# Weight scalings placed behind a unit's copies, down weights' steps and S4 operands moved, in a gated feed-forward and S4 kernel

## The chip, the cores and the metric

The kernel runs on one core of a Trainium2 chip. The metric is the time of one execution in microseconds (us) on the device. A core has engines with queues of their own: PE (TensorE, matmuls; PEld are its weight loads), DVE (VectorE), ACT (ScalarE), POOL (GpSimd) and SP (SyncE, which here only issues DMA transfers). Each works through its instructions in order, and semaphores tie them together. Matmuls write to eight PSUM banks, all else lies in SBUF.

## The reference

The input is x with 2048 tokens of 1024 values. With xn = layernorm(x) the output is x + S4(xn) + FFN(xn).

```python
Wg, Wu, Wd = (dequantize(q, scale, zero) for q, scale, zero in ...)   # int4, groups of 64
def dequantize(W_q, scale, zero):
    w = stack([W_q >> 4 & 15, W_q & 15], axis=-1).reshape(out, 2 * half)
    return (w.reshape(out, -1, 64) - zero[:, :, None]) * scale[:, :, None]

g = einsum('bsh,ih->bsi', xn, Wg)          # hidden 1024 -> 2752
u = einsum('bsh,ih->bsi', xn, Wu)
ffn = einsum('bsi,hi->bsh', silu(g) * u, Wd)   # 2752 -> 1024

# S4: a kernel K of length 1024 from 64 complex states (Cauchy sums at the roots of unity), then
y = irfft(rfft(xn, n=2048) * rfft(K, n=2048))[..., :1024] + D * xn    # causal convolution along the hidden axis
```

## The kernel before, in words

Every float32 operand is split into a high and a low float16 part, and a product is three matmul passes (high by low, low by high, high by high). The big products go through a 2 by 2 block scheme of seven products instead of eight (`PROD` names the operands' combinations).

**First stage, to about 133 us.** Sixteen tiles of x are normalised (`norm_stat`, `norm_hi`, `norm_lo`), combined into the scheme's sums (`combine`), and the first two blocks of gate and up weights are used without the scheme (`gate_up_plain`).

**Gate-and-up loop, about 133 to 883 us.** Blocks j = 2 to 20, in two halves of the tokens, cp = 0 and 1. A *unit* is one `gate_up(j, cp)` (line 595), 38 in all, in the order (2,0), (3,0), (2,1), (3,1), (4,0), (4,1), and so on to (20,1). It is seven products of twelve 128x512 matmuls. Their order on PE is 1, 7, then product 4 of the unit before (`rest(0)`), 6, then product 3 of the unit before (`rest(1)`), 2, 5. Between them ACT makes copies from bank to bank that start the next sums: B<-A after product 1 (line 617; `heads`), hb<-C after 7, D<-B after 6, a silu in place on A after 2, and one on the D of the unit before. Product 6 can't start before B<-A is done, product 5 not before D<-B. `tails` holds the DVE addition after product 5; `lag(n)` makes a generator wait until n further units have been written down.

**Weights.** A *granule* gi is half of a block's gate and up weights; block j has 2j and 2j+1. `load_w` (line 409) takes one through: `unpack` (DMA of packed rows `raw` and of scales and zeros `sz`, two DVE shifts into `w`), `scale_c` (three POOL operations on `sz`), `scale_a` (16 ACT instructions of 128x64, one for each group: w times scale plus bias; 0.43 us each in the mean), `sums` (four DVE operations), `w_hi` (two ACT casts to `nat`), `w_lo` (two DVE subtractions) and `w_t` (two transposing DMAs from SP, wf<-nat). In the loop there is one buffer for `w`, there are two for `sz`, four for `raw`, five for `nat`, four for `wf` (two blocks). Granules 4 to 7 are traced ahead of the loop, 8 to 41 in it; granule 4's unpacking is tied behind the last norm operation of tile 13 (`BEHIND`). `w_scale` cuts the 16 scalings into 5, 6 and 5, all tied behind the B<-A copy of one unit. Two further granules (`G_WP`) hold the last 64 columns' down weights.

**Down weights.** `load_wd(u)` (line 460), ten generators of some eleven steps, prepares them for the second stage; it fetches packed rows and transposed scales (w<-SZT), dequantises on DVE (`dequant`), and makes seven combinations `nd` (ACT cast, DVE subtraction, DMA store WD<-nd). The loop takes four steps after each pass (j, cp) from j = 4 on.

**S4.** The generator `s4()` builds K in the same loop, two or three steps a pass from j = 4. `s4_cauchy(qt)` (line 736), run four times, fetches cosine and sine rows (s4n<-in_csrow) into a `nat` buffer, works on them with DVE up to a reciprocal and multiplies on PE (s4s).

**Second stage, from 883 us.** The S4 convolution (cv, cc) and the last tiles, then the down product in the seven-product scheme (A, D, E with operands g and b).

**Order.** The program is traced, and a planner that simulates the time lays out each engine's queue: what was traced earlier goes first among what is ready by its reckoning. `issue_after(ins)` adds that the instructions in its block stand behind `ins` on that engine; it places nothing directly behind it. Ahead of the loop, DVE, ACT and SP work in an order written out by hand ("pinned").

Of the kernel before, what the change touches and what calls it, by code (L numbers as in the profile page):

```python
# [42 lines left out]
G_WP = G_WD + 2 * NPAIR  # L43


S4_FROM, WD_FROM = 4, 4


SPG = 8
FETCH = {8: 15, 9: 15}  # L50
BEHIND = {4: 13}

XS = 64.0
WS = 1024.0
# [33 lines left out]
def build(nc, tc, x, xp, raw_d, sz_d, par_d, vct_d, tab_d, csrow_d, out):  # L88
# [3 lines left out]
    with es:  # L92
# [193 lines left out]


        with ea:
            slots, heads, tails, ends = {}, {}, [], [None]
            rawt = {}  # L290

            def load_raw(gi):
# [27 lines left out]
            def scale_c(gi, sz):  # L320

                G.tensor_scalar(sz[:, 0], sz[:, 0], WS, None, ALU.mult)  # L322
                G.tensor_tensor(sz[:, 1], sz[:, 1], sz[:, 0], ALU.mult)
                G.tensor_scalar(sz[:, 1], sz[:, 1], -1.0, None, ALU.mult)
                return sz

            def scale_a(w, sc, groups=range(16)):

                wv = w.rearrange("p a b -> p (a b)")
                for g in groups:  # L330
                    A.activation(
                        wv[:, 64 * g : 64 * g + 64], wv[:, 64 * g : 64 * g + 64].bitcast(I32), AF.Identity,
                        bias=sc[:, 1, g : g + 1], scale=sc[:, 0, g : g + 1],
                    )
# [46 lines left out]
                w, sz = unpack(gi)  # L381
                made[gi] = w, scale_c(gi, sz)

            def w_scale(gi, part, behind=None):
                with tc.issue_after(heads[behind].ins) if behind in heads else nullcontext():
                    scale_a(*made[gi], range((0, 5, 11)[part], (5, 11, 16)[part]))

            def w_sums(gi):
                sums(made[gi][0], False)
# [16 lines left out]
                    last[0] = SP.dma_start_transpose(wf[:, 14 * k : 14 * k + 14], nat.rearrange("p a b c -> p (a b c)"))  # L406
                wt.setdefault(gi // 2, []).append(wf)

            def load_w(gi, behind=None):
                if gi in BEHIND:  # L410
                    with tc.issue_after(los[BEHIND[gi]].ins):
                        w, sz = unpack(gi)
                    made[gi] = w, scale_c(gi, sz)
                else:
                    w_unpack(gi)
                for part in range(3):
                    w_scale(gi, part, behind)
                w_sums(gi)
                w_hi(gi)
                w_lo(gi)  # L420
                w_t(gi)


            def wp_hi(i):
                made[G_WP + i] = made[G_WP + i][0], wtemp("nat", [P, 1024], F16, f"wph{i}")
                w, hi = made[G_WP + i]
                A.copy(hi, w.rearrange("p a b -> p (a b)")[:, :1024])

            def wp_lo(i):
                w, hi = made.pop(G_WP + i)  # L430
                lo = wtemp("nat", [P, 1024], F16, f"wpl{i}")
                V.tensor_tensor(lo, w.rearrange("p a b -> p (a b)")[:, :1024], hi, ALU.subtract)
                SP.dma_start(WPN[:, i, 0:1024], hi)
                SP.dma_start(WPN[:, i, 1024:2048], lo)

            def scales_t():

# [22 lines left out]
            def load_wd(u):  # L460
# [51 lines left out]
                    ready_wd[ga] = fetch_wd(ga)  # L512
                    yield
                ready_wd[gb] = fetch_wd(gb)
                yield from lag(2 if u == 0 else 1)
                ma = ready_wd.pop(ga)
                with tc.issue_after(tails[-1].ins):
                    dequant(*ma)
# [73 lines left out]

            pending = []

            def gate_up(j, cp, wf):

                def prod(i, ps, start, stop):
                    fa, fb = PROD[i]
                    xt = xtile(cp, fb)
                    for kt in range(4):  # L600
                        for n, (wi, xi) in enumerate(PASS):
                            ends[0] = PE.matmul(
                                ps, wf[kt // 2][:, 14 * (kt % 2) + 2 * fa + wi, :], xt[:, xi, kt, :],
                                start=(start and kt == 0 and n == 0), stop=(stop and kt == 3 and n == 2),
                                skip_group_check=not start,
                            )

                def rest(i):
                    if len(pending) > i:
                        pending[i]()  # L610

                nm = f"{j}_{cp}"
                isc = 1.0 / (XS * WS)
                add, mult = ALU.add, ALU.mult
                bA, bB = bank("A" + nm), bank("B" + nm, "B")
                prod(1, bA, True, True)
                heads[j, cp] = A.copy(bB, bA)
                bC = bank("C" + nm)
                prod(7, bC, True, True)
                tag = "h" if j % 2 else "e"  # L620
                hb = htile("hb_" + nm, tag)
                A.copy(hb, bC)
                rest(0)
                prod(6, bB, False, True)
                bD = bank("D" + nm, "D")
                A.copy(bD, bB)
                rest(1)
                pending.clear()
                prod(2, bA, False, True)
                A.activation(bA, bA, AF.Silu, scale=isc)  # L630
                prod(5, bD, False, True)
                tails.append(V.tensor_tensor(hb, bD, hb, add))

                def fourth():
                    prod(4, bC, False, True)
                    ha = htile("ha_" + nm, tag)
                    A.copy(ha, bC)
                    V.tensor_tensor(ha, bB, ha, add)
                    V.scalar_tensor_tensor(ha, ha, HS * isc, bA, mult, mult)
                    pending[1] = lambda: third(ha)  # L640

                def third(ha):
                    prod(3, bD, False, True)
                    A.activation(bD, bD, AF.Silu, scale=isc)
                    V.scalar_tensor_tensor(hb, hb, HS * isc, bD, mult, mult)
                    finish_h(j, cp, ha, hb)

                pending.extend((fourth, None))
# [87 lines left out]
            def s4_cauchy(qt):  # L736

                work = wtemp("nat", [P, 3, 256], F32, f"s4n{qt}")
                cs, sn, di = (work[:, i] for i in range(3))
                re, im = slice(0, 64), slice(64, 128)  # L740
                SP.dma_start(cs, csrow_d[0, 256 * qt : 256 * qt + 256].partition_broadcast(P))
                SP.dma_start(sn, csrow_d[1, 256 * qt : 256 * qt + 256].partition_broadcast(P))
                yield
                V.tensor_scalar(sn, sn, sm[:, 28:29], None, ALU.mult)
                V.scalar_tensor_tensor(di, cs, sm[:, 30:31], sn, ALU.mult, ALU.add)
                V.tensor_scalar(cs, cs, sm[:, 29:30], None, ALU.mult)
                yield
                V.tensor_tensor(sn, cs, cs, ALU.mult)
                for rows, d2 in ((re, di), (im, cs)):
                    V.tensor_tensor(d2[rows], di[rows], di[rows], ALU.mult)  # L750
                    V.tensor_tensor(sn[rows], sn[rows], d2[rows], ALU.add)
                yield
                V.reciprocal(sn, sn)
                V.tensor_tensor(sn[re], cs[re], sn[re], ALU.mult)
                V.scalar_tensor_tensor(sn[im], di[im], -1.0, sn[im], ALU.mult, ALU.mult)
                yield from lag()
                rr = sn.rearrange("p (a b) -> p b a", b=8)
                ps = bank(f"s4s{qt}")
                rows = slice(32 * qt, 32 * qt + 32)
                with tc.issue_after(ends[0].ins):  # L760
                    for l1 in range(8):
                        PE.matmul(ps[rows, 8 * l1 : 8 * l1 + 8], rr[:, l1, :], cf, start=True, stop=True)
                yield
                V.tensor_copy(s4p[rows, 48:112], ps[rows, 0:64])
                yield
# [220 lines left out]
            wd_steps = (None for u in range(NPAIR) for _ in load_wd(u))  # L986
            s4_steps = s4()

            gate_up(2, 0, wt[2])
            gate_up(3, 0, wt[3])  # L990
            for j in range(2, NJ):
                if 3 <= j < NJ - 1:
                    load_w(2 * j + 2, (j - 1, 1))
                    load_w(2 * j + 3, (j - 1, 1))
                for cp in range(2):
                    if cp or j > 3:
                        gate_up(j, cp, wt[j])
                    for _ in range(4 if j >= WD_FROM else 0):
                        next(wd_steps, 0)
                    for _ in range(3 - cp if j >= S4_FROM else 0):  # L1000
                        next(s4_steps, 0)
                if j == NJ - 2:
                    for i in range(2):
                        w_unpack(G_WP + i)
                        for part in range(3):
                            w_scale(G_WP + i, part)
                        wp_hi(i)
                        wp_lo(i)
            settle()
            for steps in (wd_steps, s4_steps):  # L1010
                for _ in steps:
# [393 lines left out]
```

## Time and profile before

| what | us |
|---|---|
| median of three runs (1336.7 to 1338.47) | 1338.17 |
| profiled execution, its own time | 1336.8 |
| its span, first to last instruction | 1335.0 |
| TensorE busy | 1277.1 |
| VectorE busy | 991.1 |
| ScalarE busy | 669.1 |
| mean granted TensorE clock | 0.987 |
| ACT scalings w<-w,sz, 640 | 217.1 |

In a row of a timeline the first number is the start in us from the span's start, the second the duration in us; then come engine, operation, written and read tiles, shapes, the number of instructions merged, and in brackets the idle time of the engine just ahead and what ended it ("issue": nothing that the profile can name). A row of the waits has the total in us, how often, and the longest. Idle time of an engine matters only where TensorE comes to wait for it.

### The profile page before, as it was taken

To read this page: it belongs to the slowest core of one execution; us is meant where nothing else is said; L and a number is where in the kernel's file an instruction comes from. 1 tells how busy PE (TensorE), PEld (TensorE's weight loads), DVE (VectorE), ACT (ScalarE), POOL (GpSimd) and SP (SyncE) were. 2 spreads that over 40 slices of the span, in tenths; PEclk is the share of its full clock that TensorE was granted. 3 is DMA by queue.
4 is the path that set the end of the run, shared out by engine and by line. 5 is a ranking of instruction groups with operands and counts; after the bars stand their busy time and mean duration, and the time that the engine had idled before them with its cause. 6 is when DMAs were issued, how large, how long until landed. Compare 5 with 4: busy or idle time off the path is not lost. (4 is left out here: it accounts for less than half of the span.)

```text
span 1335.0 us, 20888 instructions
## 1 busy us (share of the span) xinstructions
PE 1277.1 (96%) x7880; PEld 751.0 (56%) x7880; DVE 991.1 (74%) x1344; ACT 669.1 (50%) x1208; POOL 189.7 (14%) x267
## 2 busy tenths in 40 slices
PE   6999799999999989989989999999999999999998
PEld 5644344444444434434433444456557888888887
DVE  7759986568797787779668687662738897779792
ACT  4777457647664745557466756720204433443330
POOL 3220010100000100111001001000000022255540
PEclk8999899999999998999999999999999999999999
DMA  6792947459896988699789979695937779799991
GB/s 224 181 189 52 218 137 137 124 142 234 193 257 160 236 204 226 156 226 239 185 222 226 242 191 223 201 281 183 329 132 296 259 201 270 241 260 265 288 189 50
DMA packets 358400, 276.02 MB, mean 207 GB/s; under 512 B 211668, under 2 KB 304668, under 8 KB 354204
## 3 DMA queue, kind: packets, MB, share of 16 engines
q1 hardware_dynamic: 335676, 261.59, 71.4%
q0 software_dynamic: 21760, 10.49, 6.6%
q10 hardware_dynamic: 864, 2.62, 0.6%
q8 instruction: 61, 1.00, 0.3%
q14 instruction: 39, 0.32, 0.1%
HBM read 132.36 MB, written 94.84 MB: 170 GB/s over the span
## 5 line engine op out<-in xcount | busy, mean ns | idle before, releaser
L77 PEld LDWEIGHTS <-wf 128*128 128x128 f16 x3960 | 374.1, 99 | 473.7 <-issue 40.6
L77 PEld LDWEIGHTS <-g 128*128 128x128 f16 x2940 | 287.6, 98 | 33.5 <-issue 0.2
L77 ACT ACTIVATE w<-w,sz 128x64 f32<-128x64 int32 x640 | 217.1, 426 | 64.1 <-DVE w L77 54.4
L77 PE MATMUL A<-x,wf 128*128 128x512 f16 x912 | 216.7, 384 | 13.9 <-DMA wf<-nat 13.1
L77 PE MATMUL D<-x,wf 128*128 128x512 f16 x912 | 214.3, 382 | 10.3 <-ACT D L77 9.7
L77 PE MATMUL C<-x,wf 128*128 128x512 f16 x912 | 210.2, 381 | 1.2 <-ACT hb L77 1.2
L77 DVE TENSOR_TENSOR w<-w 128x256 f32<-128x256 f32 (+2 forms) x272 | 139.0, 527 | 77.6 <-ACT w L77 71.3
L77 ACT CAST g<-a 128x2560 f16<-128x2560 f32 x42 | 97.5, 2324 | 180.8 <-PE cv L77 51.2
L77 PE MATMUL A<-b,g 128*128 128x256 f16 x1680 | 185.9, 273 | 0.0
L77 DVE TENSOR_TENSOR g<-a,g 128x2560 f16<-128x2560 f32 x42 | 118.3, 2819 | 30.9 <-ACT g L77 30.9
L1257 POOL DMA_DIRECT2D out<-o x64 | 78.7, 2105 | 342.7 <-DVE o L77 334.2
L322 POOL TENSOR_SCALAR sz<-sz 128x16 f32<-128x16 f32 x42 | 29.6, 705 | 685.3 <-DMA sz<-in_sz 588.5
L77 PE MATMUL B<-x,wf 128*128 128x512 f16 x456 | 108.1, 388 | 9.6 <-ACT B L77 9.5
L77 ACT CAST nd<-w 128x896 f16<-128x896 f32 x70 | 63.5, 933 | 67.0 <-DVE w L77 56.0
L77 PE MATMUL D<-b,g 128*128 128x256 f16 x840 | 94.0, 273 | 0.0
L77 ACT CAST nat<-w 128x896 f16<-128x896 f32 x76 | 68.1, 936 | 46.0 <-issue 31.2
L77 DVE TENSOR_TENSOR nd<-w,nd 128x896 f16<-128x896 f32 x70 | 75.2, 1082 | 21.4 <-ACT nd L77 21.3
L77 DVE TENSOR_TENSOR nat<-w,nat 128x896 f16<-128x896 f32 x76 | 80.2, 1085 | 13.9 <-ACT nat L77 13.8
L77 PEld LDWEIGHTS <-x 128*128 128x128 f16 x576 | 52.4, 98 | 23.8 <-issue 2.7
L77 DVE SCALAR_TENSOR_TENSOR p<-cv,p 128x512 f32<-128x512 f32 x32 | 21.9, 686 | 49.5 <-PE cv L77 47.7
L77 PE MATMUL cv<-band,x 128*128 128x512 f16 (+3 forms) x384 | 57.0, 299 | 0.0
L77 PE MATMUL g<-x,wf 128*128 128x128 f16 (+1 forms) x336 | 48.5, 292 | 1.5 <-ACT wf L82 0.8
(145 smaller groups left out, 1199.6 us busy)
## 6 DMA issues: line engine op xcount, KB each, us to landing
a<-HF SPq DMA_DIRECT2D x28, 1280.0 KB, 8.0
WD<-nd SPq DMA_DIRECT2D x70, 448.0 KB, 4.2
b<-WD SPq DMA_DIRECT2D x49, 640.0 KB, 6.0
w<-SZT SPq DMA_DIRECT2D x80, 256.0 KB, 5.5
raw<-in_raw SPq DMA_DIRECT2D x65, 256.0 KB, 3.5
HF<-ha SPq DMA_DIRECT2D x54, 256.0 KB, 3.3
HF<-s SPq DMA_DIRECT2D x40, 256.0 KB, 3.5
HF<-hb SPq DMA_DIRECT2D x36, 256.0 KB, 3.1
```

Of the source, the lines that this page charges most:

```text
L77: return method(*args, **kw)
L322: G.tensor_scalar(sz[:, 0], sz[:, 0], WS, None, ALU.mult)
L1257: G.dma_start(dst, o[:, q], accum_op=ALU.add)
```

## The change

It moves work; what is computed stays. The 16 scalings of a granule are written down in two halves, tied behind two copies of a unit, and the rest of the granule behind a third. A generator `w_flow` does this: each `gate_up` hands it three marks, the copy B<-A, the copy D<-B and the silu of A (the first unit hands none, the second begins with D<-B). Halves of 8 scalings go behind D<-B and the silu, casts behind the next unit's B<-A. So each unit takes one granule on by a whole turn, granules 8 to 41 and then the two of `G_WP`. The next granule's rows are fetched when the second half of scalings has been written down.

The down weights' steps begin at the pass (3,0), three a pass up to j = 9 and four from then on, and the forced wait for a new unit ahead of a dequantisation is a plain step for all but the first generator. In S4 the rows are used a unit after they are fetched, and the small matmuls come two units after the reciprocal. Granule 4's unpacking is tied behind tile 15 instead of 13, its POOL scalings behind tile 15's statistics.

```diff
-S4_FROM, WD_FROM = 4, 4
+S4_FROM, WD_FROM = 4, (3, 0)
-BEHIND = {4: 13}
+BEHIND = {4: 15}
...
-            def w_scale(gi, part, behind=None):
-                with tc.issue_after(heads[behind].ins) if behind in heads else nullcontext():
-                    scale_a(*made[gi], range((0, 5, 11)[part], (5, 11, 16)[part]))
+            def w_scale(gi, groups=range(16)):
+                scale_a(*made[gi], groups)
...
                 if gi in BEHIND:
                     with tc.issue_after(los[BEHIND[gi]].ins):
                         w, sz = unpack(gi)
-                    made[gi] = w, scale_c(gi, sz)
+                    with tc.issue_after(rs[15, 0].ins):
+                        made[gi] = w, scale_c(gi, sz)
...
+            def w_flow():
+                order = list(range(8, 2 * NJ)) + [G_WP, G_WP + 1]
+                for n, gi in enumerate(order):
+                    w_unpack(gi)
+                    for groups in (range(8), range(8, 16)):
+                        mark = yield
+                        with tc.issue_after(mark.ins):
+                            w_scale(gi, groups)
+                    if n + 1 < len(order):
+                        rawt[order[n + 1]] = load_raw(order[n + 1])
+                    if gi < G_WP:
+                        w_sums(gi)
+                    mark = yield
+                    with tc.issue_after(mark.ins):
+                        (w_hi if gi < G_WP else wp_hi)(gi)
+                    if gi < G_WP:
+                        w_lo(gi)
+                        w_t(gi)
+                    else:
+                        wp_lo(gi)
+                while True:
+                    yield
...
                 ready_wd[gb] = fetch_wd(gb)
-                yield from lag(2 if u == 0 else 1)
+                if u == 0:
+                    yield from lag(2)
+                else:
+                    yield
...
-                heads[j, cp] = A.copy(bB, bA)
+                seed = A.copy(bB, bA)
+                if len(started) > 1:
+                    side.send(seed)
...
-                A.copy(bD, bB)
+                seed = A.copy(bD, bB)
+                if len(started) == 1:
+                    next(side)
+                if started:
+                    side.send(seed)
...
-                A.activation(bA, bA, AF.Silu, scale=isc)
+                seed = A.activation(bA, bA, AF.Silu, scale=isc)
+                if started:
+                    side.send(seed)
+                started.append((j, cp))
...
                 SP.dma_start(sn, csrow_d[1, 256 * qt : 256 * qt + 256].partition_broadcast(P))
-                yield
+                yield from lag()
...
-                yield from lag()
+                yield from lag(2)
                 rr = sn.rearrange("p (a b) -> p b a", b=8)
...
             for j in range(2, NJ):
-                if 3 <= j < NJ - 1:
-                    load_w(2 * j + 2, (j - 1, 1))
-                    load_w(2 * j + 3, (j - 1, 1))
                 for cp in range(2):
                     if cp or j > 3:
-                        gate_up(j, cp, wt[j])
-                    for _ in range(4 if j >= WD_FROM else 0):
+                        gate_up(j, cp, wt[j], w_steps)
+                    for _ in range((4 if j > 9 else 3) if (j, cp) >= WD_FROM else 0):
                         next(wd_steps, 0)
-                if j == NJ - 2:
-                    for i in range(2):
-                        w_unpack(G_WP + i)
-                        for part in range(3):
-                            w_scale(G_WP + i, part)
-                        wp_hi(i)
-                        wp_lo(i)
```

More of the change, by code (lines that the diff above doesn't have):

```diff
@@ L288, in build @@
         with ea:
-            slots, heads, tails, ends = {}, {}, [], [None]
+            slots, started, tails, ends = {}, [], [], [None]
             rawt = {}
@@ L407, in w_t, with load_w @@
                 wt.setdefault(gi // 2, []).append(wf)
-            def load_w(gi, behind=None):
+            def load_w(gi):
                 if gi in BEHIND:
@@ L412, in load_w @@
                         w, sz = unpack(gi)
-                    made[gi] = w, scale_c(gi, sz)
+                    with tc.issue_after(rs[15, 0].ins):
+                        made[gi] = w, scale_c(gi, sz)
                 else:
                     w_unpack(gi)
-                for part in range(3):
-                    w_scale(gi, part, behind)
+                w_scale(gi)
                 w_sums(gi)
@@ L421, in load_w, with wp_hi, wp_lo @@
                 w_t(gi)
-            def wp_hi(i):
-                made[G_WP + i] = made[G_WP + i][0], wtemp("nat", [P, 1024], F16, f"wph{i}")
-                w, hi = made[G_WP + i]
+            def w_flow():
[20 more added lines that the diff above has]
+                    yield
+            def wp_hi(gi):
+                made[gi] = made[gi][0], wtemp("nat", [P, 1024], F16, f"wph{gi}")
+                w, hi = made[gi]
                 A.copy(hi, w.rearrange("p a b -> p (a b)")[:, :1024])
-            def wp_lo(i):
-                w, hi = made.pop(G_WP + i)
-                lo = wtemp("nat", [P, 1024], F16, f"wpl{i}")
+            def wp_lo(gi):
+                w, hi = made.pop(gi)
+                lo = wtemp("nat", [P, 1024], F16, f"wpl{gi}")
                 V.tensor_tensor(lo, w.rearrange("p a b -> p (a b)")[:, :1024], hi, ALU.subtract)
-                SP.dma_start(WPN[:, i, 0:1024], hi)
-                SP.dma_start(WPN[:, i, 1024:2048], lo)
+                SP.dma_start(WPN[:, gi - G_WP, 0:1024], hi)
+                SP.dma_start(WPN[:, gi - G_WP, 1024:2048], lo)
             def scales_t():
@@ L593, in build, with gate_up @@
             pending = []
-            def gate_up(j, cp, wf):
+            def gate_up(j, cp, wf, side):
                 def prod(i, ps, start, stop):
@@ L987, in build @@
             s4_steps = s4()
-            gate_up(2, 0, wt[2])
-            gate_up(3, 0, wt[3])
+            w_steps = w_flow()
+            gate_up(2, 0, wt[2], w_steps)
+            gate_up(3, 0, wt[3], w_steps)
             for j in range(2, NJ):
-                if 3 <= j < NJ - 1:
-                    load_w(2 * j + 2, (j - 1, 1))
-                    load_w(2 * j + 3, (j - 1, 1))
                 for cp in range(2):
                     if cp or j > 3:
-                        gate_up(j, cp, wt[j])
-                    for _ in range(4 if j >= WD_FROM else 0):
+                        gate_up(j, cp, wt[j], w_steps)
+                    for _ in range((4 if j > 9 else 3) if (j, cp) >= WD_FROM else 0):
                         next(wd_steps, 0)
@@ L1001, in build @@
                         next(s4_steps, 0)
-                if j == NJ - 2:
-                    for i in range(2):
-                        w_unpack(G_WP + i)
-                        for part in range(3):
-                            w_scale(G_WP + i, part)
-                        wp_hi(i)
-                        wp_lo(i)
             settle()
```

## The prediction

> **What bounds the kernel now.** I read the page first: TensorE is busy nearly throughout, so only its holes and slow stretches can be won.
>
> ```profile
> span 1335.0 us, 20888 instructions
> PE 1277.1 (96%) x7880; PEld 751.0 (56%) x7880; DVE 991.1 (74%) x1344; ACT 669.1 (50%) x1208; POOL 189.7 (14%) x267
> ```
>
> Then the windows, to place the holes. From 900 us to the last stretch TensorE has none (100.00 of 100.00), so the second stage can gain nothing. The gate-and-up loop (about 133 to 883 us) has them all:
>
> ```profile
> 134.00:167.00 33.00, 25.94 (x100) 10.10 (x101) 30.61 (x38) 14.91 (x23) 0.00 (x0) 0.84 1.02 218
> 500.00:600.00 100.00, 91.14 (x417) 40.17 (x417) 76.03 (x152) 57.58 (x128) 10.62 (x13) 0.97 0.82 205
> 900.00:1000.00 100.00, 100.00 (x672) 60.48 (x672) 45.97 (x64) 6.93 (x6) 0.00 (x0) 1.00 0.63 219
> ```
>
> (Columns: stretch, length, busy us of PE, PEld, DVE, ACT, POOL, granted clock, DMA share, GB/s.) The table of waits says who is late:
>
> ```profile
> ACT nd L77 <- DVE w L77: 56.0, 21, 7.8
> ACT w L77 <- DVE w L77: 54.4, 25, 6.0
> PE A L77 <- DMA wf<-nat: 13.1, 12, 3.3
> PE D L77 <- ACT D L77: 9.7, 7, 4.1
> PE B L77 <- ACT B L77: 9.5, 4, 3.4
> ```
>
> TensorE waits for ScalarE's copies between banks, ScalarE in its own order for VectorE. Of the 13.1 us on weight transposes, 7.54 lie before 150 us (1.58, 1.32, 0.80, 0.56, 3.28) and 5.56 in the loop. Last, the timelines around the large holes, TensorE first, then ScalarE, then VectorE:
>
> ```profile
> 385.12 1.16 PE L77 MATMUL s4s<-s4p,s4n 128*32 128x8 f32 x16 [2.85 <-DVE s4n L77]
> 386.22 4.12 PE L77 MATMUL A<-x,wf 128*128 128x512 f16 x12
> 502.64 5.28 PE L77 MATMUL D<-x,wf 128*128 128x512 f16 x12 [4.11 <-ACT D L77]
> 578.66 2.75 PE L77 MATMUL B<-x,wf 128*128 128x512 f16 x12 [2.82 <-ACT B L77]
> 678.20 4.39 PE L77 MATMUL B<-x,wf 128*128 128x512 f16 x12 [3.42 <-ACT B L77]
> 794.69 4.44 PE L77 MATMUL B<-x,wf 128*128 128x512 f16 x12 [2.71 <-ACT B L77]
> ```
>
> ```profile
> 571.05 5.41 ACT L77 ACTIVATE w<-w,sz 128x64 f32<-128x64 int32 x16
> 576.37 1.76 ACT L77 CAST nd<-w 128x896 f16<-128x896 f32 x2
> 578.04 0.57 ACT L77 COPY B<-A 128x512 f32<-128x512 f32 x1
> 498.17 1.78 ACT L77 CAST nd<-w 128x896 f16<-128x896 f32 x2 [9.11 <-issue]
> ```
>
> ```profile
> 490.21 0.35 DVE L77 TENSOR_SCALAR s4n<-s4n,s4p 128x256 f32<-128x256 f32 x1 [6.42 <-DMA s4n<-in_csrow]
> ```
>
> Twelve matmuls take 2.75 us when the clock is up; what a row has above that I count as lost with the hole. At 578, 678 and 794 a run of 16 scalings (5.41 us) stands ahead of the copy that TensorE needs: 2.82 + (3.42 + 1.64) + (2.71 + 1.69) = 12.3 us. At 502 VectorE had stood 6.42 us for S4's cosine rows; the cast at 498.17, put down to "issue", starts 0.08 us after a VectorE operation on w ends, so it is that delay handed on: 4.11 + 2.53 = 6.6. At 385 TensorE waited for S4's own result: 2.85 + 1.37 = 4.2. With the 0.46 before a D product at 492.5, S4 costs 11.3 us.
>
> **The change part by part.**
>
> *Scalings.* The same 16 for each granule. Instead of one run placed anywhere after a B copy, there are two of 8 (half of 5.41: 2.7 us), one after a unit's copy D<-B, one after its silu of A; casts follow the next copy B<-A. A product takes 2.59 us from start to start. From the silu of A to the point where the next B copy must be done there are four products (5, 1, 7 and the fourth of the unit before): 10.4 us, of which ScalarE needs 0.56 + 2.7 + 0.57 = 3.8. The 6.6 us left also take the longest wait of a scaling for VectorE, 6.0. Queued behind a late scaling are the copies and silus; TensorE waits for them only past that reserve. The three holes should go: between 0 and 12.3 us, I take 11, as 6.0 against 6.6 leaves little if a cast stands there too.
>
> *Transposes of a finished granule.* Casts now stand right behind the B copy. Unit (11,1) of before shows such a unit: casts 1.5 and 2.4 us after its B copy at 514.9, transposes issued at 3.6 and 5.2, the last landed at 10.1. The next unit reads them 15.5 us after that copy (seven products of 2.59, less the first). Reserve 5.4 us. In (10,1), where the late ones cost 1.00 + 0.92 us, they were issued at 9.8 and 12.2. Gain between 0 and 5.6; I take 3.
>
> *Granule's rows fetched a unit ahead.* Two SP transfers per granule move ahead, past the unit's stores and the down weights' loads. ScalarE waited only 6.0 us on the POOL scalings of sz, 3 times, so this is worth at most that and lies inside the term above. Granule 9 is fetched twice (ahead, and again by its FETCH entry): 256 and 16 KB more on SP's queue, a landing of 3.5 us, hidden by a unit of 18.1 us before it is read; uncovered it would cost those 3.5 once.
>
> *S4.* Its cosine rows get a unit (18.1 us) for a landing of 4.3 us (median), the small matmuls two units after the reciprocal. The work stays in the loop: following the steps, S4 ends at unit (15,0) instead of (13,0), before the loop's end at (20,1). Between 0 and 11.3; I take 10. The price is that its working tile keeps one of five nat buffers for four units at a time. I find one cast in the loop held by a store (0.79 us, at 551.6), so I charge nothing; with a hole like 502 from it, 6.6 each. The Trainium skill ("Trainium Kernel Development and Optimization", Best Practices) warns that consistent bubbles can mean that SBUF ran out. By that rule the longer hold would be the expensive half of this edit, one 6.6 us hole per quarter of S4, 26 us; the row of 0.79 us speaks against it, and the sum goes without.
>
> *Down weights.* First step at the pass (3,0) instead of (4,0), 3 steps a pass to j = 9, then 4, and the forced wait for a new unit is a plain step. The last step falls in (19,0) instead of (20,0). Five steps still lie between asking for a granule's scales and using them: 1.25 to 1.67 units, 23 to 30 us, against a landing of 5.5. No cost; without that cover, the 29.2 us that VectorE waits for these rows today would rise.
>
> *Granule 4* is unpacked after tile 15's last norm operation (VectorE, 101.87 us) instead of about 85.8, its POOL scalings after tile 15's statistics. Granule 5 is not held and takes the earlier place; in granule 5's old place the last subtraction ends at 124.4, and the transposes were issued only at 130.95. Cover 6.5 us. Without it, each us late is one us more on TensorE, which has waited for these transposes since 133. Taken as 0, bounds -4 (ScalarE's 12 scalings between tile 15's two norm operations, 4.07 us, are gone) and +6.
>
> *The new order.* The planner lays out the whole loop again. Holes that none of the edits names are 8.2 us today (5.59 for D, 0.58 for B, 1.24 and 0.76 for the h copies). Such holes will fall elsewhere, and some more, since ScalarE still waits over 100 us for VectorE: +7, two of the size of 578 with some slow clock; bounds -4 and +20 (three like 502).
>
> Sum: -11 - 3 - 10 + 0 + 7 = -17. The profiled execution took 1336.8 us around its span of 1335.0; the median of the three runs is 1.4 higher: 1338.2 - 17 = **1321 us**.
>
> On the slow clock: the rows say that the hole of 2.71 us at 794 was followed by twelve matmuls in 4.44, that of 2.82 at 578 by 2.75. The Trainium skill ("TensorE: Matmul & The Clock Gate", What's actually happening) has the clock halve after about 3.4 us idle. By it only 502 and 678 would pay, the scalings' loss would be 10.6 instead of 12.3, and the forecast 1.7 us higher.
>
> **Rivals.**
>
> *Weights land late (slower).* A granule for odd places can no longer be ready early: today's order often issued its transposes within 1.2 us of the B copy ((17,1), (19,1)), the new one not before about 3.6. If VectorE's sums are late, as at 719.60, where the cast waited 6.80, the reserve of 5.4 us is gone, in unit after unit. For it too: the four sums (0.42 us each, 1.7) have only 5.18 - 0.56 - 2.7 = 1.9 us from the scalings' end to the next B copy, on an engine that is busy three quarters of the time. Against: the 5.4 us of reserve come behind that. It decides from 21 / 17 = 1.2 us per pair of granules, where it eats the 21 us of scalings and S4; at 2 us each, 34 - 21 = +13: 1351.
>
> *Hole for hole (same).* Copies come in time, but the re-laid order makes as many new holes: +24 instead of +7, 1338. For it: VectorE is 74 to 84% busy here and sets ScalarE's pace. Against: the large holes have two named causes, both removed.
>
> *All of it (much faster).* 12.3 + 5.6 + 11.3 = 29 gained and nothing new: 1309; with the -4 of the first stage 1305.
>
> *Half.* The scalings' holes reappear behind casts, only S4 counts: -10 + 7 = -3, 1335.
>
> **How the numbers follow.** The forecast (1312 to 1328) 0.44, all of it 0.14, half 0.08, hole for hole 0.06, late weights 0.28. A measurement of this kernel tells about 0.2%, 2.7 us, from no change. Faster 0.44 + 0.14 + 0.08 = 0.66, same 0.06, slower 0.28. The range leaves out a third of "all of it" below and about half of the slow case above: 1304 to 1346; the forecast's own range is 1312 to 1328.
>
> **What would show it.** Right: scalings in runs of 8 only, no B copy behind 16; no VectorE wait of several us for in_csrow; no s4s wait; wf waits in the loop below 3 us; TensorE's slices all 9 between 200 and 880 us. Wrong: PE A waiting for wf in most odd units; first C products after 150 us; many waits of nat casts on WD stores; or the same 30 us of bank copies late in other places.

## The result, and the profile after

The changed kernel takes 1338.66 us (median of 20 runs, 1336.47 to 1342.02) beside 1335.76 us for the kernel before (20 runs): ratio 1.0025, 95% interval 1.0017 to 1.0033. It is slower by a quarter of a percent; 1321 was forecast. Its profiled execution took 1337.9 us, the span is 1336.2 us.

TensorE's waits in the loop (150 to 884 us) of the kernel after; the columns are the total in us, how often, the longest:

```profile
PE A L77 <- DMA wf<-nat: 15.6, 10, 3.0
PE D L77 <- ACT D L77: 8.0, 4, 4.2
PE D L77 <- DVE hb L77: 3.3, 4, 1.0
PE C L77 <- DVE ha L77: 3.3, 2, 2.0
PE A L77 <- ACT ha L77: 2.2, 1, 2.2
PE C L77 <- ACT hb L77: 1.9, 1, 1.9
PE B L77 <- ACT B L77: 1.4, 2, 0.9
```

Together 35.7 us, against 30.1 in the same stretch before. The waits for B fell from 9.5 to 1.4. But the runs of 16 scalings, which the prediction had down as gone, are not: the generator `w_flow` takes 36 granules through, and 28 of them ran in halves of 8, eight as one run of 16. Both waits for B that are left stand behind such a run: 0.44 us at 653.51, with two casts in between, and 0.93 us here (ScalarE, then TensorE):

```profile
547.85 5.41 ACT L77 ACTIVATE w<-w,sz 128x64 f32<-128x64 int32 x16
553.17 0.57 ACT L77 COPY B<-A 128x512 f32<-128x512 f32 x1
```

```profile
553.79 2.75 PE L77 MATMUL B<-x,wf 128*128 128x512 f16 x12 [0.93 <-ACT B L77]
```

TensorE now waits for weights instead, 15.6 us against 5.6. VectorE in the same stretch of the kernel after:

```profile
DVE w L77 <- DMA raw<-qn: 33.0, 7, 9.4
DVE s4n L77 <- DMA s4n<-in_csrow: 19.7, 4, 9.0
```

Before, these were 0.4 and 7.1 us, with 29.2 us on w<-SZT, the other rows of a down granule, which are 0.4 here. So VectorE still waits for rows, and S4's fetch, which was to be a unit ahead, now costs almost three times as much. What one such wait does, in the timelines of VectorE, ScalarE and TensorE after:

```profile
788.49 1.22 DVE L77 TENSOR_TENSOR w<-raw,w 128x1024 f32<-128x1024 int16 x1 [9.40 <-DMA raw<-qn]
```

```profile
800.42 0.94 ACT L77 CAST nd<-w 128x896 f16<-128x896 f32 x1 [10.31 <-DVE w L77]
801.27 1.77 ACT L77 CAST nat<-w 128x896 f16<-128x896 f32 x2
802.95 0.57 ACT L77 COPY ha<-C 128x512 f32<-128x512 f32 x1
803.42 0.58 ACT L77 COPY D<-B 128x512 f32<-128x512 f32 x1
```

```profile
804.06 4.28 PE L77 MATMUL D<-x,wf 128*128 128x512 f16 x12 [4.21 <-ACT D L77]
```

VectorE stands 9.4 us, a cast waits 10.3 us for its sums, two more casts and a copy queue behind it ahead of D<-B, and TensorE stands 4.2 us and then runs twelve matmuls in 4.28 instead of 2.75 us. It is the hole of 502 us again, from another late row.

One thing improved that the sum had at 0: ahead of the loop proper (130 to 160 us) TensorE loses 7.7 us instead of 12.2. I count as lost what the starts of consecutive matmuls are further apart than 0.216 us (2.59 / 12); so slow matmuls count too. The wait of 3.28 us for a transpose at 146.68 in the kernel before is not there. Counted in the same way, the loop from 150 to 884 us loses 49.7 us instead of 42.8. That is 6.9 us more there and 4.5 less ahead of it, and the span grew by 1.2 us.

### The profile page after: what moved, and what is told of

Same layout as the page of the kernel before. It is cut to its first block, busy times and chain, and to the rows that moved or that the text cites. A ratio compares the mean times of both kernels' runs of the same rounds, so it can differ in the third digit from the quotient of the medians.

```text
span 1336.2 us, 20890 instructions
## 1 busy us (share of the span) xinstructions
PE 1275.5 (95%) x7880; PEld 749.9 (56%) x7880; DVE 991.6 (74%) x1344; ACT 670.6 (50%) x1208; POOL 187.3 (14%) x267
## 5 line engine op out<-in xcount | busy, mean ns | idle before, releaser
L77 PE MATMUL A<-x,wf 128*128 128x512 f16 x912 | 214.1, 382 | 23.2 <-DMA wf<-nat 20.9
L77 PE MATMUL D<-x,wf 128*128 128x512 f16 x912 | 213.9, 383 | 11.6 <-ACT D L77 8.0
L322 POOL TENSOR_SCALAR sz<-sz 128x16 f32<-128x16 f32 x42 | 25.9, 617 | 692.3 <-DMA sz<-in_sz 652.4
L77 PE MATMUL B<-x,wf 128*128 128x512 f16 x456 | 104.8, 379 | 1.4 <-ACT B L77 1.4
L77 DVE TENSOR_TENSOR w<-raw,w 128x1024 f32<-128x1024 int16 x20 | 24.4, 1219 | 38.6 <-DMA raw<-qn 33.0
```

The lines of the kernel that those rows point to most:

```text
L77: return method(*args, **kw)
```

## The experiments

Theories ahead of the first runs: *starved VectorE* (casts and transposes are late because VectorE waits for rows), *deadline* (the new places of scalings and casts make the transposes late by themselves), *lottery* (each new order scatters). Times in this table are ratios to the kernel before, run beside on the same chip; the other columns are us of wait between 150 and 884 us in one profile each: TensorE for wf; TensorE for ScalarE's B and D; VectorE for w<-SZT, raw<-qn and in_csrow together.

| kernel | ratio, 95% interval | median us | wf | B, D | rows |
|---|---|---|---|---|---|
| before | 1 | 1335.8 | 5.6 | 19.3 | 43.4 |
| changed | 1.0025, 1.0017 to 1.0033 | 1338.7 | 15.6 | 9.4 | 56.8 |
| scal_alone | 1.0068, 1.0052 to 1.0085 | 1345.8 | 32.6 | 3.9 | 59.8 |
| down_undone | 1.0051, 1.0037 to 1.0064 | 1344.2 | 24.6 | 5.5 | 52.5 |
| s4_undone | 1.0063, 1.0045 to 1.0082 | 1346.7 | 16.3 | 14.9 | 73.4 |
| down_alone | 0.9979, 0.9966 to 0.9993 | 1334.4 | 7.8 | 9.6 | 44.4 |
| before_fence | 0.9875, 0.9855 to 0.9894 | 1318.9 | 2.3 | 6.8 | 10.2 |
| after_fence | 0.9903, 0.9882 to 0.9924 | 1325.4 | 16.7 | 1.6 | 23.3 |
| after_fence2 | 0.9862, 0.9839 to 0.9886 | 1318.6 | 17.0 | 1.1 | 2.7 |
| after_turn | 1.0021, 1.0010 to 1.0032 | 1339.8 | 1.8 | 24.6 | 57.2 |
| before_fence2 | 0.9910, 0.9893 to 0.9928 | 1325.3 | 8.1 | 9.9 | 11.6 |
| before_fence2_down | 0.9808, 0.9792 to 0.9823 | 1311.7 | 6.7 | 3.5 | 13.0 |
| after_turn_fence2 | 0.9712, 0.9695 to 0.9729 | 1298.7 | 2.6 | 2.4 | 2.2 |
| turn_fence2_g4 | 0.9730, 0.9717 to 0.9744 | 1301.8 | 0 | 2.0 | 3.6 |

### The parts of the change

**scal_alone**: the changed kernel without its down and S4 parts.

```diff
-S4_FROM, WD_FROM = 4, (3, 0)
+S4_FROM, WD_FROM = 4, (4, 0)
...
-                if u == 0:
-                    yield from lag(2)
-                else:
-                    yield
+                yield from lag(2 if u == 0 else 1)
...
                 SP.dma_start(sn, csrow_d[1, 256 * qt : 256 * qt + 256].partition_broadcast(P))
-                yield from lag()
+                yield
...
-                yield from lag(2)
+                yield from lag()
                 rr = sn.rearrange("p (a b) -> p b a", b=8)
...
-                    for _ in range((4 if j > 9 else 3) if (j, cp) >= WD_FROM else 0):
+                    for _ in range(4 if (j, cp) >= WD_FROM else 0):
```

> The changed kernel with the down weights' steps and the S4 waits as they were before, so the scalings behind a unit's copies (and granule 4 behind tile 15) stay. Theory 'starved VectorE' (casts are late because VectorE stands behind late rows: 33.0 us for raw<-qn and 19.7 us for s4n in the changed kernel, 6.7 and 7.1 before): both waits fall back to under 10 us each, TensorE's wait for wf in the loop falls from 15.6 to under 8 us, and the time is 8 to 15 us under that of the kernel before. Theory 'deadline' (casts that must follow the B copy make the transposes late by themselves): wf stays at 12 us or more and the time is within 4 us of the changed kernel's, that is 0 to 6 us over before. Theory 'lottery' (each new order of the planner scatters by some us with no pattern): anything from -5 to +5 us, the wf wait not tied to VectorE's waits.

Slower still, 0.68%. Its wait for wf is the largest of all:

```profile
PE A L77 <- DMA wf<-nat: 32.6, 23, 5.5
```

'Starved VectorE' as I had put it fell: VectorE's long wait for raw<-qn (56.7 us) is there without the new down steps. The scalings do to B and D what was forecast (19.3 to 3.9 us), although 17 of the 36 granules ran as one run of 16 here, and lose more on wf than that (5.6 to 32.6). This is the part that costs; the two others win some of it back.

**down_undone** puts back only the down weights' three edits of that diff, **s4_undone** only the two in S4.

> The changed kernel with the down weights' steps alone put back (from pass (4,0), four a pass, forced wait for a new unit). 'Starved VectorE': the raw<-qn wait of VectorE falls from 33.0 to under 10 us, the wf wait of TensorE from 15.6 to about 10, the time 4 to 8 us under the changed kernel's. 'Deadline': raw<-qn falls, wf stays at 12 or more, time unchanged within 2 us. 'Lottery': -5 to +5 us with no tie.

> The changed kernel with S4's waits put back (rows used at the next step, small matmuls one unit later). 'Starved VectorE': the s4n wait stays between 7 and 20 us, since how early the rows are asked for is set by SP's queue and not by where the use is written; the time is within 3 us of the changed kernel's. If writing the use a unit later had worked and something else is to blame, s4n rises above 20 us and the time by 5 us or more. 'Lottery': -5 to +5 us.

Both are slower than the changed kernel (1.0051 and 1.0063 against 1.0025). So neither part is to blame. The S4 part helps the time although VectorE's wait for S4's own rows is larger with it (19.7 us) than without (8.9). VectorE's waits for all rows together are smaller with it (56.8 against 73.4), and so are TensorE's for B and D (9.4 against 14.9); what ties these to the S4 edit is open.

**down_alone**: the down steps in the kernel before.

```diff
-S4_FROM, WD_FROM = 4, 4
+S4_FROM, WD_FROM = 4, (3, 0)
...
-                yield from lag(2 if u == 0 else 1)
+                if u == 0:
+                    yield from lag(2)
+                else:
+                    yield
...
-                    for _ in range(4 if j >= WD_FROM else 0):
+                    for _ in range((4 if j > 9 else 3) if (j, cp) >= WD_FROM else 0):
```

> The kernel before with the down weights' steps alone changed. 'Starved VectorE': the raw<-qn wait rises from 6.7 to 20 us or more, the time rises 3 to 8 us over before. 'Deadline': raw<-qn rises, but casts have no deadline here, so the time stays within 2 us of before. 'Lottery': -5 to +5 us.

0.2% faster; raw<-qn does not rise (6.6 us, 7.1 before). 'Starved VectorE' is wrong on where raw<-qn comes from.

### Why VectorE waits for rows

VectorE's queue as the planner laid it out gives the reason. A pair's generator asks for the rows of its second granule, then dequantises the first, tied behind a unit's closing addition, and three steps after that the second, tied to nothing. In the queue of the kernel before, the second granule's dequantisation stands ahead of the first's in all ten pairs; presumably the planner reckons its rows there and finds nothing better to do. In the changed kernel it is so in six of ten. The same holds for S4: its use is written a unit later, but nothing ties it, and in VectorE's queue it stands soon after the fetch, as before. On the chip the rows are not there, since SP's queue runs late. SP and then VectorE of the changed kernel:

```profile
337.47 7.04 SPq L77 DMA_TRANSPOSE wf<-nat  x2
344.60 0.54 SPq L77 DMA_DIRECT2D HF<-ha  x1
345.20 1.09 SPq L77 DMA_DIRECT2D w<-SZT  x2
346.33 1.32 SPq L77 DMA_TRANSPOSE raw<-qn  x1
347.70 1.25 SPq L77 DMA_DIRECT2D s4n<-in_csrow  x2
```

```profile
341.87 1.32 DVE L77 TENSOR_TENSOR w<-w 128x256 f32<-128x256 f32 x3
352.14 0.35 DVE L77 TENSOR_SCALAR s4n<-s4n,s4p 128x256 f32<-128x256 f32 x1 [8.95 <-DMA s4n<-in_csrow]
```

VectorE came to S4's operation at 343.2; the rows were asked for only at 347.7, behind two transposes that held SP for 7 us. The new theory, *reordering*: the cure is a tie in the queue, not a later place in the text.

**before_fence**, and **after_fence** the same in the changed kernel:

```diff
-                dequant(*mb)
+                with tc.issue_after(tails[-1].ins):
+                    dequant(*mb)
```

> The kernel before, with the dequantisation of a pair's second granule tied behind the last unit's closing VectorE addition, as the first one's is. In VectorE's queue of before the second granule's comes ahead of the first's in all ten pairs, straight after its rows were asked for. Theory 'reordering' (VectorE waits for rows just asked for because the planner pulls work ahead that is written later): VectorE's wait for w<-SZT falls from 29.2 to under 8 us and the time by 2 to 6 us. Theory 'slack' (VectorE's waits here cost TensorE nothing): the wait falls as well, the time stays within 2 us. Theory 'lottery': -5 to +5 us whatever the waits do.

> The changed kernel with the same tie. 'Reordering': VectorE's wait for raw<-qn falls from 33.0 to under 8 us, and with casts earlier TensorE's wait for wf in the loop from 15.6 to about 10; time 4 to 8 us under the changed kernel's, 1 to 5 us under before. 'Deadline' (casts bound to the B copy are too late by themselves): the first wait falls, wf stays at 12 or more, time within 3 us of the changed kernel's. 'Lottery': -5 to +5 us.

In both queues all ten pairs now stand in order. The kernel before gains 1.25% from this alone (1318.9 us), rows 43.4 to 10.2 us; TensorE's waits in the loop halve, 30.1 to 15.2. So these waits of VectorE did cost TensorE, against 'slack', and much more than the lottery's 5 us. The changed kernel gains as much (1325.4), yet wf stays at 16.7: the wait for weights does not hang on VectorE's wait for these rows. 'Deadline' holds for that part.

**after_fence2** ties S4's use as well:

```diff
-                V.tensor_scalar(sn, sn, sm[:, 28:29], None, ALU.mult)
-                V.scalar_tensor_tensor(di, cs, sm[:, 30:31], sn, ALU.mult, ALU.add)
-                V.tensor_scalar(cs, cs, sm[:, 29:30], None, ALU.mult)
+                with tc.issue_after(tails[-1].ins):
+                    V.tensor_scalar(sn, sn, sm[:, 28:29], None, ALU.mult)
+                    V.scalar_tensor_tensor(di, cs, sm[:, 30:31], sn, ALU.mult, ALU.add)
+                    V.tensor_scalar(cs, cs, sm[:, 29:30], None, ALU.mult)
```

> The run before it, with S4's first three VectorE operations on the fetched rows also tied behind the last unit's closing addition, so that the rows do lie a unit ahead of their use in the queue and not only in the text. 'Reordering': VectorE's wait for in_csrow falls from 19.7 to under 4 us, the time a further 2 to 5 us. 'Deadline' and 'slack': the wait falls, time unchanged within 2 us. 'Lottery': -5 to +5 us.

VectorE's wait for in_csrow is gone altogether:

```profile
348.11 1.32 SPq L77 DMA_DIRECT2D s4n<-in_csrow  x2
363.15 0.34 DVE L77 TENSOR_SCALAR s4n<-s4n,s4p 128x256 f32<-128x256 f32 x1
```

The rows are used 13.7 us after SP had done asking for them. The median falls by 6.7 us, 1325.4 to 1318.6, though the two intervals overlap (0.9882 to 0.9886). wf stands at 17.0, four fifths of TensorE's remaining 20.9. The longest of these waits, 5.52 us until 713.60, shows what is late: the granule's scalings ran as one run of 16 from 693.22, 3.3 us behind a B copy (689.94) and not ahead of it as the change means them to, its casts followed at 701.68, and its transposes were issued from 707.77 on.

**before_fence2** has both ties and S4's new waits in the kernel before.

> The kernel before with both ties and S4's new waits: second dequantisation behind the last unit's closing addition, S4's rows fetched a unit ahead and their first use tied as well. Scalings, down weights' steps and granule 4 as before. 'Reordering': VectorE's waits for w<-SZT, raw<-qn and in_csrow together under 10 us; time 3 to 6 us under the run with one tie (1318.9), about 1314. TensorE's wait for wf in the loop under 5 us, its B waits for runs of 16 scalings still there (2 to 6 us). 'Slack': within 2 us of 1318.9. 'Lottery': within 5 us of it either way.

A miss: 1325.3, slower than with the one tie (1318.9). The wait for in_csrow did not fall (6.8 us; one of 5.0 and one of 1.7), and wf rose from 2.3 to 8.1. The tie keeps S4's use behind the unit's closing addition, but nothing keeps the fetch ahead of it: here SP asked for two of the four sets of rows at 366.6 and 446.3, after the closing additions to which their uses are tied (365.6 and 441.2), and these are the two that were waited for. Why wf rose was not traced. So S4's tie goes with a gain of 6.7 us in one order and a loss of 6.4 in another: a few us each way are within what a new order does.

**before_fence2_down** adds the down steps to that.

> The run before it plus the down weights' new steps: everything of the change but the scalings and granule 4, with both ties. Against the changed kernel with both ties (1318.6) it prices the scalings behind a unit's copies. If those cost time by late transposes ('deadline'), this is 3 to 10 us faster than 1318.6 with wf under 6 us (17.0 there). If they are worth what the forecast said once VectorE is free, it is 3 us or more slower, with B waits over 5 us (1.1 there). 'Lottery': -5 to +5 us with no tie to these waits.

1311.7, 1.0% under the run before it. Against after_fence2 it lacks only the scalings behind a unit's copies and granule 4's new place: it is 7 us faster, with wf 6.7 against 17.0 and B and D 3.5 against 1.1. The scalings as placed by the change cost time even when VectorE has its rows. 7 us is little more than the 6.4 that a new order alone has just cost; that it is the scalings rests on wf, where the difference lies, and on the runs that follow.

### Why the weights are late

**after_turn** moves a granule's three marks on by one: halves behind B<-A and D<-B, casts behind the silu of A in the same unit.

```diff
                 seed = A.copy(bB, bA)
-                if len(started) > 1:
-                    side.send(seed)
+                if len(started) == 1:
+                    next(side)
+                if started:
+                    side.send(seed)
...
                 seed = A.copy(bD, bB)
-                if len(started) == 1:
-                    next(side)
                 if started:
                     side.send(seed)
```

> The changed kernel with a granule's three marks moved on by one: first half of scalings behind B<-A, second behind D<-B, casts behind the silu of A of the same unit, some 5 us ahead of the next B copy. 'Deadline': TensorE's wait for wf in the loop falls from 15.6 to under 7 us with B and D waits not above 10, time 6 to 10 us under the changed kernel's, so 3 to 7 under before. 'Starved VectorE': as raw<-qn and s4n waits stay (over 40 us together), casts are as late as before, wf stays above 10, time within 3 us of the changed kernel's. 'Lottery': -5 to +5 us.

wf falls to 1.8 us, as 'deadline' says, but the time stays, since B and D waits rise to 24.6. ScalarE now seems to have scalings and casts in the way of the copies when VectorE is late, as it still is here (57.2 us of waits for rows). TensorE's waits in question:

```profile
PE B L77 <- ACT B L77: 13.0, 7, 3.2
PE D L77 <- ACT D L77: 11.6, 8, 5.3
PE A L77 <- DMA wf<-nat: 1.8, 3, 0.8
```

**after_turn_fence2** has the turn and both ties.

> The changed kernel with both ties and a granule's three marks moved on by one (scalings behind B<-A and D<-B, casts behind the silu of A). With VectorE free, casts should stand where they are tied: wf under 5 us as in the turn without ties (1.8), and the B and D waits of that run (24.6 us together) should fall under 8 if they came from VectorE being late ('reordering'): time about 1308 to 1314. If they come from the scalings standing ahead of what TensorE needs, they stay over 15 us and the time is 1318 or more. 'Lottery': 1318.6 plus or minus 5.

1298.7 us, 2.9% under the kernel before and faster than both kernels of this study. The two causes were real and hid each other: with the ties alone wf remains, with the turn alone B and D. TensorE's longest waits in the loop:

```profile
PE A L77 <- DMA wf<-nat: 2.6, 4, 0.9
PE B L77 <- ACT B L77: 2.1, 2, 1.5
PE D L77 <- DVE hb L77: 1.2, 2, 1.0
```

And the window from 500 to 600 us (columns as in the prediction), where TensorE was busy for 91.14 us before:

```profile
500.00:600.00 100.00, 99.43 (x472) 45.37 (x470) 85.52 (x166) 65.02 (x141) 16.12 (x18) 1.00 0.96 241
```

**turn_fence2_g4** puts granule 4 back.

```diff
-BEHIND = {4: 15}
+BEHIND = {4: 13}
...
-                    with tc.issue_after(rs[15, 0].ins):
-                        made[gi] = w, scale_c(gi, sz)
+                    made[gi] = w, scale_c(gi, sz)
```

> The turned kernel with both ties (1298.7), with granule 4's unpacking put back behind tile 13 and its POOL scalings untied, as before the change. TensorE loses 6 to 8 us between 130 and 160 us in every profile with granule 4 behind tile 15 and 11 to 13 us in every one without. If that part of the change is worth this by itself, the loss here is 11 to 13 us and the time 3 to 6 us above 1298.7. If the loss follows from something else in the new order, it stays at 6 to 8 us and the time within 2 us. If the loop gives the gain back, the loss rises and the time does not.

The loss between 130 and 160 us goes from 6.9 back to 12.5 us. The time goes up by 3.1 us, 0.9712 to 0.9730, but the intervals overlap (0.9717 to 0.9729), so this is not clear of noise. In every profile of this study the loss is 5.9 to 8.0 us with granule 4 behind tile 15 and 11.5 to 13.0 behind tile 13.

This run also prices the scalings. It differs from before_fence2_down in nothing but the scalings by `w_flow`, with the marks moved on, and is some 10 us faster (0.9730 against 0.9808, intervals apart). So the idea was worth 10 of the 14 us that the sum had for scalings and transposes together, once the marks were early enough and VectorE had its rows.

## Why the prediction was wrong

The sum said -17 us, and +2.9 was measured. Of these 20 us, 13 lie in the transposes (10.0 more on wf in place of -3) and about 10 in the scalings, S4 and the new order (-4.4 in place of -14); the first stage gave 4.5 back.

**Scalings: -11 forecast.** The mechanism held in the main: with them, waits for B and D went from 19.3 to 9.4 us in the changed kernel and to 3.9 alone, and B from 9.5 to 1.4. The holes of the kind at 578, 678 and 794 us shrank to 0.93 and 0.44. But "runs of 8 only" did not come true: eight of 36 granules ran as 16, since the ties of the scalings, too, say only "not before".

**Transposes: -3 forecast. This is the step that failed.** It read unit (11,1), where casts follow the B copy at once and the last transpose lands 10.1 us after it, as what the tie would give everywhere. The tie says "not before the B copy", not "right after it". In the sixteen units (4,1) to (19,1) of the changed kernel the second transpose was issued 4.1 to 18.8 us after the B copy, 11.9 in the median, where the working had 5.2 and a reserve of 5.4. In the unit (11,1) itself, B copy at 504.6 us, the casts came 10.6 us after it, held up by VectorE, which had stood 3.7 us for a down granule's rows; the transposes were issued at 13.5 and 15.4 and landed at 17.6 and 19.7, past the 15.5 at which the next unit reads them, and TensorE waited 2.22 us until 522.2. wf went from 5.6 to 15.6 us, and to 32.6 in scal_alone. It is the rival "weights land late", which I gave 0.28 and priced at +13; it came in at +2.9 with the other parts' gains beside it. Its decisive point, that the sums have only 1.9 us before the B copy, was in the text, and I let the 5.4 us behind it outweigh it. VectorE's wait for rows was only one way to be late: with that cured (after_fence2) wf is still 17.0, and scalings that run behind the B copy make the casts late in the same way. after_turn is the counter-proof: every mark one earlier, the casts by two products (5.2 us), and wf is 1.8.

**S4: -10 forecast, and failed for a reason that I had not seen.** I took a use written a unit later for a use that runs a unit later. In the queue it did not move: VectorE's wait for in_csrow went from 7.1 to 19.7 us. With a tie it is 0 in the changed kernel, and 6.8 in the order of before_fence2, where the fetch itself slid behind the tie. The other half of the edit did what was forecast: TensorE's wait for S4's own result (2.8 us before) is gone. That the S4 part still helps the changed kernel (s4_undone is 0.4% slower) is measured and not explained.

**Down weights: nothing forecast.** Alone they gave 0.2%, so the size was nearly right and the reason was not. I counted five steps between asking and use, for the first granule of a pair; the second's rows were used as soon as the planner thought them there. The 29.2 us of w<-SZT, which I took for a price already paid that the cover keeps from rising, cost more than all three holes of the scalings (12.3): a tie of one line is worth 1.25%, 17 us.

**Granule 4: 0, bounds -4 and +6.** TensorE loses 4.5 us less there (7.7 against 12.2), and the run that puts it back is 3.1 us slower, within noise. So it came out at about the lower bound; whether for the reason given there was not looked into.

**New order: +7.** Apart from the 10.0 us more on wf, TensorE's idle time in the loop changed by 35.7 - 30.1 - 10.0 = -4.4 us (without the slow matmuls behind the holes), where scalings, S4 and new order together had been put at -14. The term can't be told from the others; before_fence2, 6.4 us slower for an edit that was to help, suggests that +7 for a new order is no wild figure.

**The slow clock.** By the rule that the prediction quotes, only the holes at 502 and 678 would be followed by slow matmuls. In the granted clock of the kernel before, those at 385, 502, 678 and 794 were, and the one of 2.82 us at 578 was not, as the rows of the prediction have it; the last section shows why. In the kernel after, the hole of 4.21 us at 804 was followed by twelve matmuls in 4.28 us.

**Buffers.** The kernel before has five casts in the loop that waited for stores, 2.3 us in all, where I had found one. Casts of nd waited 17.6 us for stores in the changed kernel, but also 15.8 in scal_alone and 11.0 in s4_undone, which hold S4's tile no longer than before. So the Trainium skill's warning ("Trainium Kernel Development and Optimization", Best Practices) that bubbles can mean that SBUF ran out names a wait that did grow here, yet most of that growth is there without the longer hold of S4's tile, against which I had weighed it.

## What to carry to other kernels

When a planner lays out the queues, moving a line in the text moves its priority, not its time: look at the queue for where the consumer of a transfer ended up, and tie it there if the distance matters. A tie gives a lower bound only; before binding work behind a mark, add up what must be finished between the mark and the deadline on every engine, at the lateness that the profile shows and not at its best unit. Two faults can hide each other, so try cures together before dropping either: beside the kernel before, the change with the turn alone was 0.2% slower, with the ties alone 1.4% faster, with both 2.9%.

## What the runs showed of the hardware

**Transposing transfers hold the SP queue far longer than plain ones.** In the loop of the changed kernel a wf<-nat transpose stood in it for 2.1 us in the median (70 of them, 1.4 to 5.4), a plain transfer for 0.44 (398). The two at 337.5 took 7.0 us together, and the fetches behind them were issued only then. A fetch's landing time (median 5.7 us for S4's rows in the changed kernel) says nothing of this, because it is counted from the issue.

**What a hole does to the clock depends on how it falls.** In the traces of all fourteen kernels the granted clock changes only at steps of 3.41 us on a grid that stays fixed through a trace. Between 140 and 880 us, all 47 full-clock steps in which TensorE stood idle for 1.98 us or more were followed by a step at 0.50; of 2892 with less than 1.94 us idle only one was (the five in between went both ways). The hole of 2.82 us at 578 in the kernel before was cut by the grid, and the longer part left TensorE busy for 1.49 of 3.41 us; the shorter hole at 794 lay in one step, left 0.70 us, and was paid for in the next (stretch, length, busy us of PE, granted clock, DMA share, GB/s):

```profile
576.73:580.15 3.42, 1.49 (x7) 1.00 1.06 233
791.78:795.19 3.41, 0.70 (x4) 1.00 1.09 313
795.19:798.61 3.42, 3.42 (x10) 0.50 0.55 170
```
